# A conditional moved from between two stages to behind the last, with four vector sums and six weight loads re-spread

## The chip, the core and the metric

The kernel runs on one core of a Trainium2 chip. A core has five engines, each with its own instruction stream: TensorE (PE in the profile, its weight loads PEld), VectorE (DVE), ScalarE (ACT), GpSimd (POOL) and SyncE (SP). They meet through semaphores. DMAs are issued from the streams of SP, ACT and POOL and run on 16 DMA engines that all queues share. SP's DMAs form one queue: what is issued later lands later. The metric is the device time in microseconds (us) of one execution; lower is better.

## The reference

Two layers on `x` of 4 x 1024 tokens by 1024 channels (4096 tokens). Each layer gates its input with a two-way decayed scan over time (`_bi_wkv`); the first layer then applies a dense 1024 x 1024 product, the second an RMS norm and a mixture of experts: 32 experts with 4 chosen per token, plus one shared expert. Cut to what the change touches:

```python
logits = flat @ router_w.T
topk_w, topk_ids = lax.top_k(softmax(logits), 4)        # 4 experts for each token
gu = lax.ragged_dot(xs, w1, group_sizes)                # w1: 32 x 1024 x 1024
g, u = jnp.split(gu, 2, axis=-1)
ys = lax.ragged_dot(silu(g) * u, w2, group_sizes)       # w2: 32 x 512 x 1024
shared = (silu(flat @ sg) * (flat @ su)) @ sd           # the shared expert, all tokens
out = residual + (routed + shared)
```

All of it is float32.

## The kernel before

The 4096 tokens are cut into 8 chunks of 512. The kernel has three stages, each a stretch of straight-line code for every engine.

**Stage 1** (`run(order())`, line 932 on) makes the scans, the first layer, the router and the shared expert of chunks 0 to 5. TensorE's work there is a list of *pieces*, each an output tile of 128 x 512 that costs 16 matmul instructions: `first_ffn`, `shared_up` and `shared_down`. `run` (line 380) walks the list. For each piece it first issues the weight DMA of the piece two places further on (`early`), then the piece's matmuls (`do`), then whatever `after(n, ...)` has put n pieces later (a DVE pass that empties PSUM comes one piece later, the transposes back to rows two pieces later), and last one step of every generator in the list `beside`. The generators are the planner's side work: a bare `yield` ends a step. The order of the instructions on each engine is exactly this order of emission, because the whole stage stands in a `manual_schedule` block; nothing is moved later.

The last pieces are the sixteen of `shared_up(5)` (line 640) and the eight of `shared_down(5)` (line 667), called **U0 to U15** and **D0 to D7** here. D-piece ct loads 512 KB of `sd` weights (`wpc`, line 673, three buffers), loads the 256 KB residual tile `rT` (line 677), multiplies, lets DVE add the product into `rT` (line 694), transposes it (line 685), copies it (ACT, line 686) and writes it to `sum_d` (ACT's queue, line 687).

Beside these runs `plan` (line 705), which turns the router's choices into lists of tokens for blocks of one expert each, in *units*: a pair unit is two blocks of 128 tokens of one expert, a single unit one block. 68 pair and 12 single units are written out in the code (`WHOLE`); rarer inputs need further units. `plan` leaves the number of these further units in `many[2]`; in this input it is zero. Part-way, `plan` appends the generator `first_weights` (line 895), which loads the expert weights of the first two units: `load` (line 815) issues for a unit three DMAs of 2048 KB each on SP's queue, the two halves of `w1` (line 826, called **w1a** and **w1b** below) and `w2` (line 833). Steps of `first_weights` before: both halves of unit 0's `w1` after U14; its `w2` after U15; both halves of unit 1's `w1` after D0; its `w2` after D1.

Pair units multiply by a seven-product scheme that needs sums of weight quarters. `sums_up` (line 838, instructions at line 845) makes those of a unit's `w1` with four DVE subtractions over 128 x 2048 elements, which read both halves of `w1`. For unit 0 they stand after the end of the pieces (lines 938 and 939).

**Between the stages** (line 1243) stands `with tc.If(count(2, ...) > 0)`. Every engine loads `many[2]` into a register (line 1226), compares and branches. The body holds the further units (`extra`), and then loads the first two units' weights, unit 0's sums and unit 0's tokens again, since the further units used their places. With zero further units each engine jumps over it, and on the way brings its semaphores to the values that the body would have left; what comes behind waits for those.

**Stage 2** (`run_units`, line 1170) works through the 80 units: transposes of the gathered tokens (line 980, copied by ACT at line 981), the up products, the down products (line 1126 for pairs), and an accumulating scatter into `sum_d`. Unit 0's tokens were gathered during `plan`; those of unit 1 are gathered by POOL (line 878) when stage 2 starts.

**Stage 3**, at the end, makes the shared expert of chunks 6 and 7 (line 1421 on), copies finished rows of `sum_d` to `out`, and adds the last two chunks in SBUF (`sums[j]`, line 1463), from where ACT's queue writes them to `out` (line 1464).

Of the kernel before, what the change touches and what calls it, by code (L numbers as in the profile page):

```python
# [22 lines left out]
P = 128  # L23
CH = 512
# [7 lines left out]
def kernel(  # L32
# [15 lines left out]
    nc = tc.nc  # L48
# [5 lines left out]
    NT = B * T  # L54
# [9 lines left out]
    MAXU = (MAXB // 2, E)  # L64
    WHOLE = (68, 12)
# [11 lines left out]
    sum_d = dram.tile([NT + P, C], FP, name="sum_d")  # L77
# [11 lines left out]
        out=before, in_=before, pattern=[[1, P]], compare_op=ALU.is_gt, fill=0.0, base=0, channel_multiplier=-1  # L89
# [48 lines left out]
    for L in range(2):  # L138
# [7 lines left out]
        q = const.tile([P, NC, B], FP, name=f"rest{L}")  # L146
# [5 lines left out]
    with tc.tile_pool(name="empty", bufs=1) as pz:  # L152
# [9 lines left out]
            out=slots_d[0 : E * BPE * BLK, :].rearrange("(p r s) o -> p r s o", p=P, s=BLK), in_=nil  # L162
        )
        nc.sync.dma_start(
            out=slots_d[E * BPE * BLK :, :].rearrange("(p s) o -> p s o", p=1), in_=nil[0:1, 0, :, :]
        )

        for n in range((NT - 2 * CH) // P, NT // P, 2):
            nc.scalar.dma_start(
                out=sum_d[bass.ds(n * P, 2 * P), :].rearrange("(p r) c -> p (r c)", p=P), in_=zeros  # L170
# [192 lines left out]
    count, told = [0], [0]  # L363
# [16 lines left out]
    def run(pieces, ahead=2):  # L380
        for i, piece in enumerate(pieces):
            for p in pieces[i : i + ahead + 1]:
                if p.early:
                    p.early()
                    p.early = None
            while work["vector"] < pace[0] * work["tensor"] and mix():
                pass
            piece.do()
            work["tensor"] += piece.tensor
            count[0] += 1  # L390
            now = sorted(d for d in due if d[0] <= count[0])
            due[:] = [d for d in due if d[0] > count[0]]
            for _, _, f, vector, tensor in now:
                f()
                work["vector"] += vector
                work["tensor"] += tensor
            for stream in list(beside):
                step = next(stream, None)
                if step is None:
                    beside.remove(stream)  # L400
                else:
                    work["vector"] += step[0]
                    work["tensor"] += step[1]
# [51 lines left out]
    sums, accs = {}, {}  # L455
# [247 lines left out]
    have = {}  # L703

    def plan():
# [9 lines left out]
        with tc.tile_pool(name="plan", bufs=1, side="right") as pl, tc.tile_pool(  # L715
# [24 lines left out]
            for kind, n in enumerate((npair, nsing)):  # L740
# [50 lines left out]
                if kind == 0:  # L791
                    beside.append(first_weights())
# [17 lines left out]
    whole = []  # L810
# [4 lines left out]
    def load(unit, at):  # L815

        kind, n = unit
        e = nc.values_load(
            have["experts"][0:1, kind, n : n + 1],
            engines=[SP],  # L820
            min_val=0,
            max_val=E - 1,
            skip_runtime_bounds_check_because="worked out above from counts, and held to that range",
        )
        for k in range(2):
            nc.sync.dma_start(
                out=have["w1"][at][k],
                in_=w1[bass.ds(e, 1), k * NK * P : (k + 1) * NK * P].rearrange("e (k p) f -> p (e k) f", p=P),
            )
            if k == 0:  # L830
                yield
        yield
        nc.sync.dma_start(
            out=have["w2"][at], in_=w2[bass.ds(e, 1)].rearrange("e (k p) f -> p (e k) f", p=P)
        )
        yield

    def sums_up(at):


        (b11, b12), (b21, b22) = ((w[:, :, 0:I], w[:, :, I : 2 * I]) for w in have["w1"][at])
        t = have["t_up"]

        def op(to, x, y):
            nc.vector.tensor_tensor(to, x, y, ALU.subtract)  # L845

        op(t[3], b22, b12)
        yield
        op(b12, b12, b11)
        yield  # L850
        op(t[2], b22, b12)
        yield
        op(t[4], b21, t[2])
        yield
# [21 lines left out]
    def gather(to, i, n):  # L876

        nc.gpsimd.indirect_dma_start(  # L878
            out=to,
            out_offset=None,  # L880
            in_=h_d,
            in_offset=bass.IndirectOffsetOnAxis(ap=have["tokens"][:, i, n : n + 1], axis=0),
        )
        return to
# [8 lines left out]
        have["t_down"] = {i: pwt.tile([P, ND, 512], FP, name=f"t_down{i}") for i in (2, 3, 4)}  # L893

    def first_weights():
        for at in range(2):
            for step, _ in enumerate(load(whole[at], at)):
                if step == 1:
                    yield 0.0, 0.0
            yield 0.0, 0.0  # L900

    def order():

        pieces = first_ffn(0, False) + first_ffn(1, False) + late_gate(0)

        pieces.insert(-1, Piece(lambda: None, tensor=LATENCY / 3))
        pieces += [Piece(lambda: None, tensor=0.5) for _ in range(7)]

        def slower():
            pace[0] = PACE  # L910
            work["tensor"] = max(work["tensor"], work["vector"] / PACE)

        pieces.append(Piece(slower, tensor=0.0))
        up, gates = shared_up(0), late_gate(1)
        for i, piece in enumerate(up):
            pieces.append(piece)
            if i % 2 == 1:
                pieces.append(gates.pop(0))
        pieces += gates
        pieces += shared_down(0) + shared_up(1) + shared_down(1)  # L920
        pieces += first_ffn(2, True) + first_ffn(3, True) + shared_up(2) + shared_down(2) + shared_up(3)
        for b in range(2, B):
            q = NCH * b

            pieces += first_ffn(q, True) + first_ffn(q + 1, True)
            if b + 1 < B:
                pieces += shared_down(q - 1) + shared_up(q)
            else:
                pieces += shared_down(q - 2) + shared_up(q - 1) + shared_down(q - 1)
        return pieces  # L930

    with tc.manual_schedule(engines={PE, DVE, ACT, POOL, SP}):
        run(order())

        run([Piece(lambda: None, tensor=0.0) for _ in range(3)])
        while beside:
            run([Piece(lambda: None, tensor=0.0)])
        for _ in sums_up(0):
            pass

# [3 lines left out]
    with ExitStack() as m:  # L946
# [219 lines left out]
        def rest_of(s):  # L1166
            for _ in s:
                pass
# [54 lines left out]
        ENG = {PE, DVE, ACT, POOL, SP}  # L1223

        def count(at, most):
            return nc.values_load(
                many[0:1, at : at + 1],
                min_val=0,
                max_val=most,
                skip_runtime_bounds_check_because="a sum of counts, held to that range",  # L1230
            )

        def extra(kind, lo, n):
            if lo >= MAXU[kind]:
                return
            with tc.If(n > lo):
                us = [Unit((kind, i), i % 2) for i in range(lo, min(lo + 4, MAXU[kind]))]
                with tc.manual_schedule(engines=ENG):
                    run_units(us, False)
                extra(kind, lo + 4, n)  # L1240


        with tc.If(count(2, MAXU[0] + MAXU[1]) > 0):
            for kind in range(2):
                extra(kind, WHOLE[kind], count(kind, MAXU[kind]))
            with tc.manual_schedule(engines=ENG):
                for at in range(2):
                    rest_of(load(whole[at], at))
                rest_of(sums_up(0))
                for i, hs in enumerate(have["first"]):  # L1250
                    gather(hs, i, whole[0][1])

        tail = NT // CH - 2
# [90 lines left out]
        with tc.manual_schedule(engines=ENG):  # L1348
# [90 lines left out]
            sums = []  # L1439
            for j, w in enumerate(have["w1"][before_last]):  # L1440
                sums.append(w.rearrange("p k f -> p (k f)").rearrange("p (t c) -> p t c", c=C))
                nc.sync.dma_start(
                    out=sums[j], in_=sum_d[bass.ts(tail + j, CH), :].rearrange("(t p) c -> p t c", p=P)
# [39 lines left out]
            for m in range(HF):  # L1483
                i = NSI + m
# [15 lines left out]
                turn_out()  # L1500


# [1 line left out]
_VECS = {  # L1504
    "w0": "L0_cond_w",
# [52 lines left out]
```

## Time and profile before

| | |
|---|---|
| median of 3 runs | 5091.98 us (5087.41 to 5094.61) |
| the profiled execution | 5095.89 us |
| its span, first to last instruction | 5093.8 us |
| TensorE busy | 4793.8 us, 94% |
| VectorE busy | 3225.9 us, 63% |
| ScalarE, GpSimd busy | 1434.3 us, 811.1 us |
| DMA | 1071.45 MB, mean 210 GB/s |
| mean granted TensorE clock | 0.989 |

The profile gives for each engine the instructions in order of time, with the idle time before each and what ended it. A float32 matmul of 128 x 512 shows as two instructions of about 0.59 us that overlap, so that 16 of them take 7.03 us. Stage 2 begins at 1881.22 us from the start of the span, stage 3's last instruction on TensorE is at 5088.84 us. A row whose engine carries a q is of the engine's sequencer: it waits, branches or issues a DMA. The duration of an issued DMA in a row of SP is the time that SP needed to hand it to the queue, not the transfer's.

### The profile page before, as it was taken

How to read it: one execution, taken by the hardware profiler on the slowest of the kernel's cores; microseconds unless marked ns; L12 is line 12 of the kernel's file. 1: busy time of each engine (PE TensorE's matmuls, PEld its weight loads, DVE VectorE, ACT ScalarE, POOL GpSimd, SP SyncE). 2: the span in 40 equal slices, each digit the busy share in tenths (PEclk: the TensorE clock that was granted, in tenths of full speed). 3: DMA queues.
4: the chain of work that ended last, by engine and by line, in shares of the span. 5: the costliest groups of instructions: out<-in, count | busy, mean ns of one | idle time of the engine just before them, and what ended most of it. 6: DMA issues, size and time to landing. Idle time of an engine off the chain costs nothing.

```text
span 5093.8 us, 36409 instructions
## 1 busy us (share of the span) xinstructions
PE 4793.8 (94%) x12810; PEld 2220.2 (44%) x12810; DVE 3225.9 (63%) x3416; ACT 1434.3 (28%) x1833; POOL 811.1 (16%) x765
## 2 busy tenths in 40 slices
PE   0479999999899979999999999999999999999999
PEld 0124444444444434444444444444444444444444
DVE  9988988888752226565656565565656565656434
ACT  5557656566441101111111111111111111111100
POOL 0113202401222101111111111111111111111100
PEclk9979999999999989999999999999999999999999
DMA  4678679669678356767676767676767767676633
GB/s 156 188 203 217 189 227 278 165 203 285 176 204 229 118 196 218 232 220 232 217 238 215 238 214 239 216 237 216 237 215 238 225 228 225 227 226 226 183 110 108
DMA packets 502209, 1071.45 MB, mean 210 GB/s; under 512 B 30433, under 2 KB 235362, under 8 KB 501186
## 3 DMA queue, kind: packets, MB, share of 16 engines
q1 hardware_dynamic: 364050, 736.31, 41.9%
q0 software_dynamic: 74656, 223.12, 20.9%
q10 hardware_dynamic: 63312, 109.59, 6.0%
q8 instruction: 104, 1.70, 0.1%
q14 instruction: 87, 0.71, 0.0%
HBM read 833.65 MB, written 205.65 MB: 204 GB/s over the span
## 4 chain that ended last, share of the span: by engine, by line
PE 63%; ACT 0%; issue 0%; DVE 0%; ACTq 0%
PE gA L1126 15%; PE gC L1126 10%; PE gB L1126 10%; PE dA L1126 8%; PE dB L1126 5%; PE dC L1126 5%; PE tr L980 2%; PE gA L1014 2%; PE gB L1014 2%; PE tr L1063 1%; PE dA L1076 1%; PE dB L1076 1%; ACT hsT L981 0%; PE tr L1461 0%; ACT y L1083 0%
## 5 line engine op out<-in xcount | busy, mean ns | idle before, releaser
L652 PE MATMUL mm<-c,wpc 128*128 128x512 f32 x1536 | 667.1, 593 | 0.0
L440 PE MATMUL mm<-c,w0t 128*128 128x512 f32 x1024 | 450.0, 601 | 206.7 <-DMA w0t<-in_w 206.7
L1126 PE MATMUL gC<-w,s_up 128*128 128x512 f32 x1184 | 532.3, 592 | 0.0
L1126 PE MATMUL gB<-t_up,s_up 128*128 128x512 f32 x1152 | 517.9, 592 | 0.0
L1126 PE MATMUL gA<-w,hsT 128*128 128x512 f32 x1088 | 489.7, 593 | 0.0
L1110 POOL DMA_INDIRECT sum_d<-y,tokens x148 | 303.6, 2052 | 920.7 <-DMA sum_d<-y,tokens 545.5
L652 PEld LDWEIGHTS mm<-c,wpc 128*128 128x128 f32 x1536 | 289.6, 190 | 355.1 <-issue 353.9
L878 POOL DMA_INDIRECT hs<-h_d,tokens x146 | 147.6, 1011 | 1636.5 <-PE tr L980 1540.6
L440 PEld LDWEIGHTS mm<-c,w0t 128*128 128x128 f32 x1024 | 196.7, 193 | 456.1 <-issue 444.5
L680 PE MATMUL mm<-sact,wpc 128*128 128x512 f32 x768 | 345.3, 604 | 14.9 <-DMA wpc<-in_sd 12.2
L1126 PEld LDWEIGHTS gC<-w,s_up 128*128 128x128 f32 x1184 | 224.8, 190 | 282.2 <-issue 282.2
L1126 PEld LDWEIGHTS gB<-t_up,s_up 128*128 128x128 f32 x1152 | 218.9, 190 | 275.5 <-issue 259.5
L845 DVE TENSOR_TENSOR t_up<-w,w 128x2048 f32<-128x2048 f32 x136 | 310.6, 2284 | 0.0
L1126 PEld LDWEIGHTS gA<-w,hsT 128*128 128x128 f32 x1088 | 201.7, 190 | 227.9 <-issue 227.9
L293 DVE TENSOR_TENSOR_SCAN fg<-decay,tail,fg 128x1024 f32<-128x1024 f32 x128 | 292.7, 2328 | 0.0
L1126 PE MATMUL dB<-t_down,s_down 128*128 128x512 f32 x544 | 256.9, 595 | 0.1
L1126 PE MATMUL dA<-w,actT 128*128 128x512 f32 x544 | 255.8, 592 | 0.0
L1126 PE MATMUL dC<-w,s_down 128*128 128x512 f32 x544 | 255.7, 592 | 0.0
L981 ACT COPY hsT<-tr 128x512 f32<-128x512 f32 x296 | 172.7, 588 | 292.8 <-PE tr L980 292.8
L1126 PE MATMUL gA<-t_up,hsT 128*128 128x512 f32 x544 | 244.5, 592 | 0.0
L1051 ACT ACTIVATE act<-c 128x512 f32<-128x512 f32 x68 | 42.9, 630 | 708.9 <-DVE c L1047 708.9
L680 PEld LDWEIGHTS mm<-sact,wpc 128*128 128x128 f32 x768 | 146.3, 195 | 189.0 <-issue 185.0
(295 smaller groups left out, 6386.3 us busy)
## 6 DMA issues: line engine op xcount, KB each, us to landing
w<-in_w SPq DMA_DIRECT2D x240, 2048.0 KB
fg<-euk POOLq DMA_DIRECT2D x64, 512.0 KB
c_d<-r ACTq DMA_DIRECT2D x64, 512.0 KB
w0t<-in_w SPq DMA_DIRECT2D x64, 512.0 KB
c<-c_d SPq DMA_DIRECT2D x120, 256.0 KB
wpc<-in_sg SPq DMA_DIRECT2D x48, 512.0 KB
wpc<-in_su SPq DMA_DIRECT2D x48, 512.0 KB
wpc<-in_sd SPq DMA_DIRECT2D x48, 512.0 KB
```

The source lines that it names most:

```text
L293: nc.vector.tensor_tensor_scan(fg[:, m, ::-1], decay[L][:, ct, b : b + 1].to_broadcast([P, T]), fg[:, m, ::-1], tail[:, m : m + 1], ALU.mu ...
L440: nc.tensor.matmul(mm, lhsT=tiles[ot][:, it, :], rhs=c0s[it], start=(it == 0), stop=(it == NC - 1))
L652: nc.tensor.matmul(mm, lhsT=wts[f, n][:, kt, :], rhs=c1s[q, kt], start=(kt == 0), stop=(kt == NC - 1))
L680: nc.tensor.matmul(mm, lhsT=wts[ct][:, f, :], rhs=acts[q, f], start=(f == 0), stop=(f == NSI - 1))
L845: nc.vector.tensor_tensor(to, x, y, ALU.subtract)
L878: nc.gpsimd.indirect_dma_start(out=to, out_offset=None, in_=h_d, in_offset=bass.IndirectOffsetOnAxis(ap=have["tokens"][:, i, n : n + 1], a ...
L980: nc.tensor.transpose(tr[:, r, :], hs[:, bass.ts(4 * q + r, P)], ident)
L981: nc.scalar.copy(self.hsT[:, 4 * q : 4 * q + 4, b, :], tr)
L1014: nc.tensor.matmul(ps, lhsT=self.hsT[:, k, 0, :], rhs=w[k // NK][:, k % NK, bass.ts(n, I)], start=(k == 0), stop=(k == NC - 1),)
L1076: nc.tensor.matmul(ps, lhsT=self.actT[:, k, 0, :], rhs=w[:, k, bass.ts(n, 512)], start=(k == 0), stop=(k == NI - 1),)
L1110: nc.gpsimd.indirect_dma_start(out=sum_d, out_offset=bass.IndirectOffsetOnAxis(ap=tokens[:, i, self.n : self.n + 1], axis=0), in_=y, in_of ...
L1126: nc.tensor.matmul(ps, lhsT=x[:, k, :], rhs=w[:, k, :], start=(k == 0 and not more), stop=(k == half - 1), skip_group_check=more,)
```

## The change

`first_weights` now issues one DMA of 2048 KB in a step: unit 0's w1a after U14, its w1b after U15, its w2 after D0; then unit 1's w1a after D1, its w1b after D3, its w2 after D5. Beside unit 1's loads, one instruction of unit 0's `sums_up` is emitted in each step: after D1, D2, D3 and D4. The loop that made the four sums behind the pieces is gone.

The conditional is gone from between the stages. One with the same condition stands behind stage 3. Its body first writes the last two chunks' rows back to `sum_d`, then does the further units, then copies all of `sum_d` to `out`; loading the first weights again is no longer needed there. With zero further units it is jumped over.

```diff
     def first_weights():
-        for at in range(2):
-            for step, _ in enumerate(load(whole[at], at)):
-                if step == 1:
-                    yield 0.0, 0.0
+
+        for _ in load(whole[0], 0):
             yield 0.0, 0.0
+        sums = sums_up(0)
+        for _ in load(whole[1], 1):
+            for _ in range(2):
+                yield (0.0 if next(sums, sums) is sums else 2.3), 0.0
 
@@ at the end of stage 1
         run([Piece(lambda: None, tensor=0.0) for _ in range(3)])
         while beside:
             run([Piece(lambda: None, tensor=0.0)])
-        for _ in sums_up(0):
-            pass
 
@@ between stage 1 and stage 2
-        with tc.If(count(2, MAXU[0] + MAXU[1]) > 0):
-            for kind in range(2):
-                extra(kind, WHOLE[kind], count(kind, MAXU[kind]))
-            with tc.manual_schedule(engines=ENG):
-                for at in range(2):
-                    rest_of(load(whole[at], at))
-                rest_of(sums_up(0))
-                for i, hs in enumerate(have["first"]):
-                    gather(hs, i, whole[0][1])
-
@@ behind stage 3
+        with tc.If(count(2, MAXU[0] + MAXU[1]) > 0):
+            for j in range(2):
+                nc.sync.dma_start(
+                    out=sum_d[bass.ts(tail + j, CH), :].rearrange("(t p) c -> p t c", p=P), in_=sums[j]
+                )
+            for kind in range(2):
+                extra(kind, WHOLE[kind], count(kind, MAXU[kind]))
+            for q in range(NT // CH):
+                nc.sync.dma_start(out=out[bass.ts(q, CH), :], in_=sum_d[bass.ts(q, CH), :])
```

## The prediction

> **What bounds the kernel now.** I read the waits of TensorE first, in two windows: from 1700 to 1885 us (the end of stage 1 and the step to stage 2), and from 1885 to 4995 us (stage 2 and most of stage 3).
>
> ```profile
> PE mm L680 <- DMA wpc<-in_sd: 12.2, 1, 12.2
> PE tr L980 <- DVEq L1243: 11.5, 1, 11.5
> PE tk_ps L797 <- DVE tokens L800: 6.1, 3, 4.7
> ```
>
> ```profile
> PE tr L980 <- ACT hsT L981: 3.5, 12, 0.3
> PE tr L1063 <- ACT hsT L981: 2.2, 12, 0.2
> PE dA L1076 <- ACT actT L1064: 0.7, 1, 0.7
> ```
>
> From 1885 us on TensorE waits 6.4 us in 3110: it bounds stages 2 and 3, so what starts stage 2 earlier ends the kernel earlier by as much. Ahead of it stand three waits of 12.2, 11.5 and 4.7 us, all within the stretch that the change touches. TensorE's rows show where (start, duration, instruction, idle before and its end):
>
> ```profile
> 1788.18 7.03 PE L680 MATMUL mm<-sact,wpc 128*128 128x512 f32 x16
> 1807.39 8.69 PE L680 MATMUL mm<-sact,wpc 128*128 128x512 f32 x16 [12.18 <-DMA wpc<-in_sd]
> ...
> 1828.74 0.49 PE L797 MATMUL tk_ps<-ident,got 128*128 128x128 f32 x1 [4.73 <-DVE tokens L800]
> 1829.03 9.75 PE L680 MATMUL mm<-sact,wpc 128*128 128x512 f32 x16
> ...
> 1867.83 1.04 PE L685 MATMUL tr<-ident,rT 128*128 128x128 f32 x8
> 1869.11 0.66 PE L685 MATMUL tr<-ident,rT 128*128 128x128 f32 x4 [0.24 <-ACT rT L686]
> 1881.22 3.78 PE L980 MATMUL tr<-ident,t_down 128*128 128x128 f32 x16 [11.46 <-DVEq L1243]
> ```
>
> These are D0, D1, the planner's transposes, D3, the last transposes and stage 2's first. D1 and D3 take 8.69 and 9.75 us instead of 7.03: TensorE ran at half clock after the idle stretch. The windows 1797 to 1807 and 1827 to 1835 show a granted clock of 0.67 and 0.57 against 1.00, and DMA engines busy at 1.04 and 1.08 of what they can, with 365 GB/s. Undisturbed, D4 to D7 follow at 7.30 us each. So the D-pieces lose 12.2 + 4.7 of waiting and 1.7 + 2.7 of slow clock, 21.3 us, and the step to stage 2 loses 11.5.
>
> The cause of the first lies in SP's queue:
>
> ```profile
> 1787.05 1.00 SPq L826 DMA_DIRECT2D w<-in_w  x2
> 1788.09 0.51 SPq L673 DMA_DIRECT2D wpc<-in_sd  x1
> 1788.79 12.65 SPq L833 DMA_DIRECT2D w<-in_w  x1
> 1801.48 0.51 SPq L673 DMA_DIRECT2D wpc<-in_sd  x1
> 1802.04 7.15 SPq L677 DMA_DIRECT2D rT<-resT_d  x1
> ```
>
> D1's weights (1788.09) stand behind 4.19 MB of unit 0's `w1`, and `rT` of D0 and D1 behind more. DVE waits for `rT`, and the planner's copies stand behind it on DVE: that is the 4.7.
>
> **A rule for landings.** D1's weights landed at 1807.4; DVE went on with `rT` of D0, D1, D2 at 1815.0, 1827.7 and 1835.8. Bytes issued up to each since 1787.05, with the 1.18 MB of POOL's gathers at 1787 to 1792: 5.90, 8.78, 13.76, 16.64 MB. The estimate 1787.05 + MB / 0.375 + 4.4 us gives 1807.2, 1814.9, 1828.1, 1835.8. I use it below.
>
> **Part 1, the loads.** SP still waits for U15 until 1787.0 before the first. The new order is w1a, D1's weights, w1b, D2's weights, `rT` D0, w2, D3's weights, `rT` D1, unit 1's w1a, D4's weights, and so on. D1's weights have 3.80 MB at most before their end: 1801.6. TensorE is idle from 1795.2, so 6.4 us instead of 12.2. The wait is long enough for the slow clock once more, so D1 takes 8.7 again, to 1810.3. D2's weights (6.42 MB): 1808.6, in time. D3's (9.30 MB): 1816.3, needed at 1817.6, when D2 ends. `rT` of D1 (9.57 MB): 1817.0, so the planner's second transpose waits only for DVE's pass and copy, 0.75 + 0.28 and hand-overs, about 0.7 us, and D3 starts at 1818.9, warm. D4's weights (12.19 MB): 1824.0, needed at 1826.2. Then 7.30 each: D7's last matmul ends at 1855.0 instead of 1867.8. **Gain 12.9 us.** The margins are 1 to 2 us. Unit 1's w1b and w2, 4.19 MB, now come after D3 and D5, when the DMA was used at 0.32 (window 1835 to 1870), and are wanted only when DVE makes unit 1's sums (1899.8 before). `rT` of D6 and D7 stand behind the last w2, with a piece of slack.
>
> On the clock the Trainium skill ("TensorE: Matmul & The Clock Gate", Part 1) says that an idle window of about 3.4 us halves it and about 3.4 us of work restore it, 1.7 us lost each time. The rows show 1.7 and 2.7. By the page the old D-pieces lose 20.3 and the gain is 11.9; by the rows 12.9. I take the rows.
>
> **Part 2, the sums.** DVE's rows before:
>
> ```profile
> 1868.76 2.28 DVE L845 TENSOR_TENSOR t_up<-w,w 128x2048 f32<-128x2048 f32 x1
> 1871.07 2.29 DVE L845 TENSOR_TENSOR w<-w 128x2048 f32<-128x2048 f32 x1
> 1873.40 2.29 DVE L845 TENSOR_TENSOR t_up<-w,w 128x2048 f32<-128x2048 f32 x1
> 1875.72 2.29 DVE L845 TENSOR_TENSOR t_up<-w,t_up 128x2048 f32<-128x2048 f32 x1
> ```
>
> 4 x 2.3 = 9.2 us, with TensorE idle. They move behind DVE's passes of D0 to D3, one in a piece of 7.3 us, where DVE has 0.75 us and the planner's few copies to do. Cost nothing, covered by the matmuls. The first waits for w1b (5.90 MB, 1807.2), and its place on DVE comes at about 1811. Were w1b late, what stands behind it is the pass of D1 and the planner's copies, and TensorE waits for these; every us late beyond 1814 would be one on the path.
>
> **Part 3, the conditional between the stages.**
>
> ```profile
> L1243 PEldq COMPARE_BRANCH  x1: 3947/3947/3947, 1870.5 to 1870.5; - x1
> L1243 SPq COMPARE_BRANCH  x1: 50/50/50, 1857.5 to 1857.5; - x1
> L1243 ACTq COMPARE_BRANCH  x1: 50/50/50, 1873.0 to 1873.0; - x1
> L1243 DVEq COMPARE_BRANCH  x1: 72/72/72, 1876.8 to 1876.8; - x1
> ```
>
> DVE branches at 1876.8 and runs its next instruction at 1881.0: the jump costs 4.1 us, and TensorE waits for what comes behind it. ACT takes 2.5 between the same points, SP 2.5, TensorE 3.9 within the branch. All this goes. What is late next is ACT: after the last matmul (time 0) its three `rT` copies with their DMA issues run from 0.6 to 3.8, its four copies for stage 2 follow, and the transposes with two buffers wait for these. That puts the fourth transpose group's end, and the first up product, at 5.9 instead of 17.0 (1867.8 to 1884.8). That product runs warm: 3.43 instead of 3.88. **Gain 11.5 us**, sums included. Lower bound 7, if the first copies also wait about 4 us for the last `sum_d` write to land. POOL's gather for unit 1, held for 81.8 us by SP's part of the jump, may go at about 1793; its 1.05 MB then move the landings by 2.8 us, past margins of 1.3 to 2.2. I take **1 us** off for it (0 to 3).
>
> **Part 4, the conditional at the end.** Now it lies behind the last instruction. TensorE ends at 5089.5; five waits 0.5, the register load 0.76 (its row at 1869.6), the branch 3.95: 5094.7, and the semaphores 0.3. DVE: last instruction sent at 5089.5, then 0.5 + 0.55 + 0.07 + 4.1: 5094.8. ACT: last DMA issued at 5090.6, then 0.35 + 0.86 + 0.05 + 2.5: 5094.4. SP and POOL have long been there and jumped. The closing barrier takes 0.9 after the last. So 5096.1 instead of 5093.8 (there it waits for the last write, landed at 5092.6): **2.3 us lost**. Here a page weighs against the change: "Runtime: NRT & Kernel Launch", Instruction fetch mechanics, says that a taken branch out of the fetched window must fetch its target first; while "Advanced Engine Details and Errata", Control Flow Timing, prices a compare-and-branch at 108 ns. By the latter the end would cost nothing, hidden by the last write. The rows at line 1243 side with the former; bounds 0 and 6 (POOL's slowest jump took 6.1).
>
> **Sum.** 12.9 + 11.5 - 1 - 2.3 = 21.1 us, of the profiled 5095.89, so 5074.8 there. That execution is 3.9 above the median; on the median, 5091.98 - 21.1 = **5071 us**.
>
> **Rivals.**
> 1. *The burst stays.* The loads still want 2.88 MB in a piece of 7.3 us, 394 GB/s, and the windows show 365 to 386. If each of D1 to D4 misses its margin, the loads' gain halves to 5: 11.5 + 5 - 1 - 2.3 = 13, giving 5079. For it: the margins of 1 to 2 us. Against: unit 1's load now runs at half the rate.
> 2. *The old wait is replaced.* Stage 2's tiles lie where stage 1's did, and wait for the last `sum_d` write: boundary 7 instead of 11.5, giving 5076. For it: ACT's row at line 1140 waits for those semaphores. Against: that wait was over at once, and the first of it comes 9 us later.
> 3. *Slower.* DVE is in order, and the first sum stands ahead of D1's pass. If w1b lands at T, D3 cannot start before about T + 3.5, against 1818.9; the gain of 21 is gone from T = 1836 on, and with T = 1850 the kernel takes 5105. Against: the same bytes landed at 1807.
> 4. *It does nothing.* The gains meet something later that was due anyway, giving 5091. Against: TensorE's 6.4 us of waits in stages 2 and 3.
>
> **How the numbers follow.** Forecast 0.66 (own range 5064 to 5076), rival 1 0.13, rival 2 0.10, rival 3 0.05, rival 4 0.06. 0.2% is 10.2 us, about what a measurement of this kernel can tell. Faster: the forecast, rival 2 and most of rival 1, 0.86; within: rival 4 and the poor end of rival 1, 0.09; slower 0.05. The range leaves out rivals 3 and 4 and some of each tail: 5063 to 5081.
>
> **What would show it.** D1 waits about 6 us, D3 starts near 1819 without a wait over 1 us; four line-845 rows between 1810 and 1845; stage 2's first transposes near 1857 with no idle above 1; branches after 5065 with 2.5 to 4 us behind them, the span ending 5 to 7 us after the last transpose. A wait over 3 us of DVE for `w`, or a wait of TensorE at line 980 for a DMA, would prove me wrong.

## The result, and the profile after

The changed kernel takes 5075.59 us (median of 8 runs, 5070.53 to 5079.3), the one before in the same runs 5092.75 (8 runs, 5087.41 to 5096.23): a ratio of 0.9967, 95% interval 0.9956 to 0.9978, or 11 to 22 us. The forecast was 5071, with a range of 5063 to 5081. The profiled execution took 5070.53 us with a span of 5068.8, against 5095.89 and 5093.8: 25 us in these two.

The two longest waits of TensorE from 1700 to 1900 us (us in total, times, longest):

```profile
PE mm L680 <- DMA wpc<-in_sd: 7.4, 1, 7.4
PE tk_ps L797 <- DVE tokens L800: 1.7, 3, 0.9
```

The wait of 11.5 us for the jump at L1243 is gone, the planner's longest fell from 4.7 to 0.9, and D1's fell from 12.2 to 7.4. TensorE's rows of the same stretch:

```profile
1785.02 7.03 PE L680 MATMUL mm<-sact,wpc 128*128 128x512 f32 x16
1799.43 9.36 PE L680 MATMUL mm<-sact,wpc 128*128 128x512 f32 x16 [7.38 <-DMA wpc<-in_sd]
...
1817.10 0.39 PE L797 MATMUL tk_ps<-ident,got 128*128 128x128 f32 x1 [0.38 <-DVE tokens L800]
1817.32 7.03 PE L680 MATMUL mm<-sact,wpc 128*128 128x512 f32 x16
...
1853.41 1.04 PE L685 MATMUL tr<-ident,rT 128*128 128x128 f32 x8
1854.48 0.44 PE L980 MATMUL tr<-ident,t_down 128*128 128x128 f32 x2
1854.75 0.60 PE L685 MATMUL tr<-ident,rT 128*128 128x128 f32 x4
1855.19 0.82 PE L980 MATMUL tr<-ident,t_down 128*128 128x128 f32 x6
...
1857.78 3.60 PE L1126 MATMUL gA<-w,hsT 128*128 128x512 f32 x8
```

D1 still starts late and runs 9.36 us instead of 7.03, so the slow clock came once more (granted clock 0.51 from 1797 to 1804 us); D3 starts without a loss and runs 7.03 (granted clock 1.00 from 1804 on). From D0's first matmul to the last transposes of the D-pieces it is 1853.41 - 1785.02 = 68.39 us, where it was 1867.83 - 1788.18 = 79.65. The first up product follows 1857.78 - 1853.41 = 4.36 us later (16.96 before). What these rows also show is that L980, an instruction of stage 2, runs *between* two groups of L685, the last of stage 1. On ACT, too, a copy of stage 2 (L981) stands between two of stage 1 (L686):

```profile
1855.13 0.59 ACT L686 COPY rT<-tr 128x512 f32<-128x512 f32 x1 [0.49 <-ACT rT L686]
1855.61 0.59 ACT L981 COPY hsT<-tr 128x512 f32<-128x512 f32 x1
...
1856.16 0.58 ACT L686 COPY rT<-tr 128x512 f32<-128x512 f32 x1
```

SP's rows (for an issued DMA the second number is the time to hand it to the queue), and DVE's rows of the four sums:

```profile
1783.88 0.40 SPq L826 DMA_DIRECT2D w<-in_w  x1
1784.33 0.50 SPq L673 DMA_DIRECT2D wpc<-in_sd  x1
1785.05 4.03 SPq L826 DMA_DIRECT2D w<-in_w  x1
1789.12 4.16 SPq L673 DMA_DIRECT2D wpc<-in_sd  x1
```

```profile
1809.44 2.29 DVE L845 TENSOR_TENSOR t_up<-w,w 128x2048 f32<-128x2048 f32 x1
...
1817.73 2.28 DVE L845 TENSOR_TENSOR w<-w 128x2048 f32<-128x2048 f32 x1
...
1823.21 2.28 DVE L845 TENSOR_TENSOR t_up<-w,w 128x2048 f32<-128x2048 f32 x1
...
1826.08 2.28 DVE L845 TENSOR_TENSOR t_up<-w,t_up 128x2048 f32<-128x2048 f32 x1
```

D1's weights (1784.33) now stand behind w1a alone, and all four sums run under matmuls. At the end of the kernel the branches stand at L1492:

```profile
L1492 PEldq COMPARE_BRANCH  x1: 4138/4138/4138, 5062.5 to 5062.5; - x1
L1492 DVEq COMPARE_BRANCH  x1: 72/72/72, 5063.8 to 5063.8; - x1
L1492 ACTq COMPARE_BRANCH  x1: 50/50/50, 5064.5 to 5064.5; - x1
```

The last piece of DVE's work starts at 5062.07 and the span ends at 5068.8, 6.73 us later. Before, it started at 5089.51 and the span ended 4.33 us later. So the end of the span is 2.4 us longer. The metric takes in a little more than the span: 5095.89 - 5093.84 = 2.05 us before and 5070.53 - 5068.80 = 1.73 after, so in the metric 2.1 of these 2.4 us are left.

**One ruler for all runs.** I cut each profiled span at four points: D0's first matmul; the last transposes of the D-pieces (so the first length is "D-pieces"); the first up product of stage 2 ("step"); the start of DVE's last instruction (the length up to it is "stages 2, 3"); the end ("tail"). The sum of the four is the time from D0 to the end.

| kernel | D0 starts at | D-pieces | step | stages 2, 3 | tail | D0 to the end |
|---|---|---|---|---|---|---|
| before | 1788.18 | 79.65 | 16.96 | 3204.71 | 4.33 | 3305.65 |
| before, again | 1786.87 | 79.53 | 16.89 | 3204.72 | 4.32 | 3305.46 |
| changed | 1785.02 | 68.39 | 4.36 | 3204.29 | 6.73 | 3283.77 |
| changed, again | 1788.73 | 68.56 | 4.36 | 3204.28 | 6.68 | 3283.88 |
| 1 loads as before | 1790.84 | 78.71 | 4.38 | 3204.28 | 6.67 | 3294.04 |
| 2 sums behind the pieces | 1788.08 | 69.39 | 4.36 | 3209.62 | 6.93 | 3290.30 |
| 3 conditional between | 1787.53 | 68.15 | 11.39 | 3205.00 | 4.33 | 3288.87 |
| 4 D1's weights first | 1788.82 | 59.51 | 4.36 | 3204.28 | 6.89 | 3275.04 |
| 4 again | 1792.95 | 60.22 | 4.36 | 3204.30 | 6.72 | 3275.60 |
| 5 no conditional | 1788.38 | 67.68 | 4.36 | 3204.28 | 5.51 | 3281.83 |
| 6 short one at the end | 1787.09 | 69.01 | 4.36 | 3204.28 | 7.00 | 3284.65 |
| 7 short one between too | 1787.91 | 68.85 | 4.36 | 3204.30 | 6.68 | 3284.19 |

From D0 on the two profiles of one kernel agree within 0.2 us (0.6 for kernel 4). The 25.0 us between the first two profiles are 11.26 of D-pieces + 12.60 of step + 0.42 in stages 2 and 3 - 2.40 of tail = 21.88, and 3.16 of a D0 that started earlier. The 0.42 is the first up product, which no longer starts at half clock (3.60 us instead of 4.04). Between kernels with the same loads (changed, 2, 3, 5, 6 and 7) the D-pieces differ more, 67.7 to 69.4 us.

### The profile page after: what moved, and what is told of

Same layout as the page of the kernel before. It is cut to its first block, busy times and chain, and to the rows that moved or that the text cites. A ratio compares the mean times of both kernels' runs of the same rounds, so it can differ in the third digit from the quotient of the medians.

```text
span 5068.8 us, 36393 instructions
## 1 busy us (share of the span) xinstructions
PE 4784.5 (94%) x12810; PEld 2216.4 (44%) x12810; DVE 3226.9 (64%) x3416; ACT 1432.7 (28%) x1833; POOL 809.8 (16%) x765
## 4 chain that ended last, share of the span: by engine, by line
PE 89%; DVE 3%; DMA 3%; ACT 3%; issue 1%; POOL 0%; SPq 0%; ACTq 0%; POOLq 0%; DVEq 0%
PE gA L1126 15%; PE mm L652 11%; PE gC L1126 10%; PE gB L1126 10%; PE dA L1126 8%; PE mm L440 7%; PE mm L680 6%; PE dB L1126 5%; PE dC L1126 5%; PE tr L980 2%; PE gA L1014 2%; PE gB L1014 2%; PE tr L1063 1%; PE tr L541 1%; DMA xg<-in_xT 1%
## 5 line engine op out<-in xcount | busy, mean ns | idle before, releaser
L680 PE MATMUL mm<-sact,wpc 128*128 128x512 f32 x768 | 343.0, 601 | 10.3 <-DMA wpc<-in_sd 7.4
L981 ACT COPY hsT<-tr 128x512 f32<-128x512 f32 x296 | 172.5, 588 | 280.9 <-PE tr L980 280.9
```

The lines of the kernel that those rows point to most:

```text
L680: nc.tensor.matmul(mm, lhsT=wts[ct][:, f, :], rhs=acts[q, f], start=(f == 0), stop=(f == NSI - 1))
L981: nc.scalar.copy(self.hsT[:, 4 * q : 4 * q + 4, b, :], tr)
```

## The experiments

The theory: the loads, the sums and the jump each give what the prediction's parts say, and D0's start varies from run to run. The rivals: one of them gives nothing by itself, the gains lie in each other's shadow, or stage 1 became faster. Diffs are against the changed kernel. All but two of the kernels compute the whole; 5 and 6 leave the further units out, which this input doesn't need.

**1. The loads as before.**

```diff
-        for _ in load(whole[0], 0):
-            yield 0.0, 0.0
-        sums = sums_up(0)
-        for _ in load(whole[1], 1):
-            for _ in range(2):
-                yield (0.0 if next(sums, sums) is sums else 2.3), 0.0
+        for at in range(2):
+            for step, _ in enumerate(load(whole[at], at)):
+                if step == 1:
+                    yield 0.0, 0.0
+            yield 0.0, 0.0
+        for _ in sums_up(0):
+            yield 2.3, 0.0
```

> The changed kernel with the six loads back in the old steps (both halves of unit 0's w1 after U14, its w2 after U15, both halves of unit 1's w1 after D0, its w2 after D1) and the four sums after D2 to D5. My theory (the burst of loads makes the waits within the D-pieces, the step to stage 2 is a gain of its own): from D0's first matmul to D7's last about 79 us again (before 79.7, after 68.4), D1 waits about 12 us for its weights, the step from D7's last matmul to stage 2's first up product stays at 4.4 us, the whole is 11 us slower than the changed kernel, about 5086. Rival (the D-pieces gained because the sums and the conditional left their end, not because of the loads): the stretch stays near 68 us and the whole near 5075.

TensorE's waits from 1700 to 1900 us:

```profile
PE mm L680 <- DMA wpc<-in_sd: 11.9, 1, 11.9
PE tk_ps L797 <- DVE tokens L800: 5.8, 3, 4.5
```

(The four sums come after D2 to D5 here.) The waits of the kernel before are back, the D-pieces take 78.71 us, and the time is 5087.17 (12 runs), 0.9985 [0.9977, 0.9994] of before. The step stays at 4.38. So the spread of the loads is worth 78.71 - 68.39 = 10.3 us by itself, and it does not touch the step.

**2. The sums behind the pieces, without a conditional there.**

```diff
-        sums = sums_up(0)
         for _ in load(whole[1], 1):
             for _ in range(2):
-                yield (0.0 if next(sums, sums) is sums else 2.3), 0.0
+                yield 0.0, 0.0
@@ behind the pieces
+        for _ in sums_up(0):
+            pass
```

> The changed kernel with unit 0's four sums behind the pieces again, where they were; the loads spread, the conditional at the end. My theory (sums and conditional lay one behind the other on DVE, but TensorE can do its transposes and the first product beside the sums): the first up product still starts 4.4 us after D7, the second waits for DVE until about 11.7 us after D7 instead of 7.8, so 4 us slower than the changed kernel, up to 6 with a dip of the clock: 5080. Rival (all of the sums' 9.2 us lies on the path): first product at 13 us or later, 9 us slower, 5085.

TensorE's rows after the step (lines behind the edit stand one further down in this kernel):

```profile
1861.84 3.60 PE L1127 MATMUL gA<-w,hsT 128*128 128x512 f32 x8
1868.80 5.40 PE L1127 MATMUL gB<-t_up,s_up 128*128 128x512 f32 x8 [3.36 <-DVE s_up L995]
```

The first product needs no sum and comes as early as in the changed kernel; the second waits 3.36 us for DVE and then runs 5.40 us instead of 3.60. It starts 11.3 us after the last transposes of the D-pieces; 11.7 was expected. The wait and the slow product are 5.2 us, and stages 2 and 3 are 5.3 us longer. The time is 5079.63 (7 runs), 0.997 [0.9959, 0.9981] of before.

**3. The conditional between the stages**, with the body of before and without the one at the end; loads and sums as in the changed kernel.

```diff
+        with tc.If(count(2, MAXU[0] + MAXU[1]) > 0):
+            for kind in range(2):
+                extra(kind, WHOLE[kind], count(kind, MAXU[kind]))
+            with tc.manual_schedule(engines=ENG):
+                for at in range(2):
+                    rest_of(load(whole[at], at))
+                rest_of(sums_up(0))
+                for i, hs in enumerate(have["first"]):
+                    gather(hs, i, whole[0][1])
@@ behind stage 3
-        with tc.If(count(2, MAXU[0] + MAXU[1]) > 0):
...
```

> The changed kernel with the conditional back between the stages with its old body, and none at the end; the loads and the sums as changed. My theory (the jump by itself costs TensorE about 6 us there: DVE's last pass 1.0, waits and register load 1.1, jump 4.1, then transposes 3.6): first up product about 10.6 us after D7 instead of 4.4, some 0.4 of slow clock, the end 2.4 us shorter, together 4 us slower than the changed kernel, 5080. Rival (the sums alone made the old step long, the jump was covered by them): first product at 5 to 6 us after D7, the end 2.4 shorter, 1 to 2 us faster than the changed kernel.

```profile
1855.68 1.04 PE L685 MATMUL tr<-ident,rT 128*128 128x128 f32 x8
1856.96 0.65 PE L685 MATMUL tr<-ident,rT 128*128 128x128 f32 x4 [0.24 <-ACT rT L686]
1863.47 3.81 PE L980 MATMUL tr<-ident,t_down 128*128 128x128 f32 x16 [5.86 <-ACTq L1243]
1867.07 4.31 PE L1126 MATMUL gA<-w,hsT 128*128 128x512 f32 x8
```

Two earlier rows, D1 on TensorE and POOL's first gather for unit 1, are used further down:

```profile
1800.88 10.17 PE L680 MATMUL mm<-sact,wpc 128*128 128x512 f32 x16 [6.32 <-DMA wpc<-in_sd]
1862.85 0.94 POOL L878 DMA_INDIRECT hs<-h_d,tokens  x1 [70.50 <-SPq L1243]
```

The step is 11.39 us instead of 4.36, and the first product runs 4.31 us instead of 3.60; the tail is 4.33 again. Between D0 and the end that is 5.1 us over the changed kernel. The time is 5077.91 (6 runs), 0.9968 [0.9955, 0.998] of before, 2.3 us over the changed kernel's median, which the intervals don't separate from 5. Of the 12.60 us by which the change shortened the step, 7.03 are the conditional's, and the other 5.57 the sums', near the 5.3 of experiment 2. How the 7.03 divide between the jump and the order that the conditional forces on the engines, no run shows.

**4. D1's weights ahead of all of unit 0's.** One more step before the first load moves the six loads one piece later; D1's weights are then issued before w1a.

```diff
     def first_weights():
+        yield 0.0, 0.0
         for _ in load(whole[0], 0):
             yield 0.0, 0.0
```

> The changed kernel with one empty step ahead of the first load, so that each load comes one piece later and D1's weights are issued ahead of unit 0's w1a. My theory (D1's wait of 7.4 us and the 2.3 us of slow clock behind it come from the one load that still stands ahead of D1's weights): no wait over 1.5 us in the D-pieces, from D0's first matmul to D7's last 59 to 61 us instead of 68.4, the rest as in the changed kernel, 8 to 9 us faster than it: 5067. Rival (the DMA engines are simply full, the wait moves to D2 or D3, or to the sums waiting for w1b): the stretch stays at 66 us or more and the gain below 3 us.

```profile
1788.82 13.90 PE L680 MATMUL mm<-sact,wpc 128*128 128x512 f32 x32
...
1802.96 7.14 PE L680 MATMUL mm<-sact,wpc 128*128 128x512 f32 x16
...
1812.02 0.39 PE L797 MATMUL tk_ps<-ident,got 128*128 128x128 f32 x1 [1.37 <-DVE tokens L800]
```

D0 and D1 are one block of 32 matmuls in 13.90 us: no wait, no slow clock (granted clock 1.00 throughout). D1's weights were issued at 1779.83 here, w1a at 1787.68. The D-pieces take 59.51 us, and the time is 5065.85 (4 runs, 5061.85 to 5074.8), 0.9947 [0.993, 0.9964] of before, whose median beside it was 5094.43. **From D0 on, this version is shorter than both kernels.** It was run once more:

> The version that issues the weights of D1 ahead of both halves of unit 0's w1, once more. If its gain over the changed kernel was not chance: the D-pieces take 59 to 61 us, and the time is 8 to 9 us below the changed kernel's, 5064 to 5068 us. If it was a favourable set of runs: 5070 to 5076 us.

The D-pieces took 60.22 us. The total, 5069.85 (4 runs), fell between the two expectations, beside 5096.19 for the kernel before: 0.995 [0.9933, 0.9966], close to the first ratio. D0 started at 1792.95 in this profile, the latest of all; from D0 on it is 8.2 to 8.8 us shorter than the changed kernel both times. In the trace, then, the gain was not chance; the total carries the start of D0 with it, and in the totals alone the intervals of this version and of the changed kernel (0.9956 to 0.9978) still overlap.

**5. No conditional at all.** The block behind stage 3 is taken out; the further units cannot be done.

```diff
-        with tc.If(count(2, MAXU[0] + MAXU[1]) > 0):
...
-            for q in range(NT // CH):
-                nc.sync.dma_start(out=out[bass.ts(q, CH), :], in_=sum_d[bass.ts(q, CH), :])
```

> The changed kernel without any conditional: it leaves out the further units, of which this input has none. My theory (the conditional at the end costs what the span shows behind DVE's last instruction, 6.7 us against 4.3): 4.3 us from DVE's last instruction to the end, 2.4 us faster than the changed kernel, 5073. Rival (the span's end is not the execution's: the closing costs elsewhere what it saves here): the tail shrinks but the time stays, 5075 to 5076.

The tail is 5.51 us, not 4.3: only half of the 2.4 us comes back. The other 1.2 us are there without any conditional. The time is 5075.82 (6 runs, 5072.02 to 5080.53), 0.9964 [0.9951, 0.9976], which lies where the rival had it but scatters too much to decide. What the execution takes outside the span was 2.48 us in the profiled execution (1.75 to 2.63 in the six runs) against 1.73 in the changed kernel, so part of what the tail saves does come back there, as the rival says.

**6. A short conditional at the end.** The body loses the further units (`extra`) and keeps ten writes, so that the jump is over a few instructions.

```diff
-            for kind in range(2):
-                extra(kind, WHOLE[kind], count(kind, MAXU[kind]))
```

> The changed kernel with the conditional at the end, but only the writes of sums and the copies to the output in its body; the further units, of which this input has none, are left out, so the jump is over a few hundred bytes of code instead of all units. My theory (the 3.5 to 4 us behind each branch are the fetch of a target far away): the branch of TensorE takes below 0.5 us, the gap behind DVE's and ACT's below 0.5, the tail is 4.5 to 5 us. Rival (a taken branch costs that much wherever it leads): TensorE's branch takes about 4 us and the tail stays at 6.7.

```profile
L1492 PEldq COMPARE_BRANCH  x1: 369/369/369, 5065.2 to 5065.2; - x1
```

The branch fell from 4.14 us to 0.37, as expected, and yet the tail is 7.00 us, not the 4.5 to 5 expected (5073.44 us, one run). So a long jump is not needed for a long tail. The transfers of the last 8 us say what is there besides. In the following rows each number is the rate in a slice of 0.2 us, in GB/s; the last slice is the span's end. The kernel before:

```profile
GB/s 0 0 18 271 289 289 294 149 0 0 0 0 0 0 0 0 0 0 0 0 0 0 184 289 289 261 269 302 289 287 287 164 0 0 0 0 0 0 0 0
```

The changed kernel, with two queues of the same view:

```profile
GB/s 0 0 0 0 0 0 0 0 0 0 248 289 284 230 305 353 271 269 264 95 20 31 100 10 5 20 23 8 0 0 0 0 0 82 41 41 0 0 0 0
...
q14 instruction: 5, 0.04, 1.7%
q8 instruction: 2, 0.03, 1.6%
```

Experiment 6, and then 5:

```profile
GB/s 0 0 0 0 0 0 0 0 20 274 287 279 246 310 271 274 269 330 51 23 20 8 8 10 8 20 23 13 0 0 0 0 0 0 0 0 0 0 0 0
```

```profile
GB/s 292 133 0 0 0 0 0 0 0 0 0 0 0 0 0 0 202 292 289 253 266 302 289 279 289 182 0 13 5 0 0 0 0 0 0 0 0 0 0 0
```

Before, the last write's bulk ends at once, in slice 32. In the changed kernel the bulk ends in slice 20, and then 1.6 us follow at mostly 5 to 31 GB/s (the 100 has two of the code packets named below in it); in experiment 6 some 2 us at 8 to 51; in 5, two slices. 289 GB/s over 16 DMA engines is 18 for one: the trickle looks like one engine of the 16 that finishes late. The queues marked `instruction` carry, by that name, code: packets of 8 and 16 KB, seven in these 8 us of the changed kernel, two in experiment 6, one in experiment 5 and none in the kernel before; the trace has the 16 KB ones at 0.93 to 1.1 us. In experiment 6 both fall into the last write (starts 5066.42 and 5067.21). That the last write waits behind a code packet on its DMA engine is likely from these times, but no run had the one without the other.

Which of the two ends the tail can be read from the DRAIN rows, with which each engine goes into the closing barrier (first and last start). The changed kernel, then experiment 6:

```profile
L1548 SPq DRAIN  x3: 7/7/13, 5067.9 to 5068.2; - x3
L1548 DVEq DRAIN  x2: 10/14/17, 5067.6 to 5068.3; - x2
```

```profile
L1546 SPq DRAIN  x3: 7/7/7, 5070.9 to 5071.1; - x3
L1546 ACTq DRAIN  x2: 8/8/8, 5067.3 to 5071.2; - x2
```

SP is the one that waits for the last write, and it is last both times. In the changed kernel DVE, the last of the engines behind a long jump, is only 0.3 us ahead of it, so jumps and write run side by side and either alone would have made most of the 2.4 us. In experiment 6 the other engines are 3.6 us ahead, and SP with the late write makes the whole tail. Of SP's 2.4 us in the changed kernel, 1.6 are the later landing (3.6 us after the hand-over to the queue instead of 2.0); the other 0.8 are the conditional's semaphores, through which SP steps behind it: the span ends 2.0 us after the landing, where it was 1.3.

**7. A short conditional between the stages**, beside the one at the end.

```diff
+        with tc.If(count(2, MAXU[0] + MAXU[1]) > 0):
+            nc.vector.tensor_copy(many[:, 0:1], many[:, 0:1])
```

> The changed kernel, with a second conditional between the stages that has the same condition and a body of one small copy on VectorE, so that every engine loads the register, compares and branches there, but over a few instructions only. Theory A (the length of the jump is what cost the time between the stages): TensorE's branch there takes under 0.5 us, the first up product of stage 2 starts 5.5 to 7.5 us after D7's last matmul (4.4 without a conditional, 11.4 with the long jump), and the clock stays full. Theory B (any conditional there costs it, by the meeting of the engines and the semaphores): 10 us or more and half clock after it. The rest is as in the changed kernel: some 5073 to 5077 us by A, 5078 to 5082 by B.

```profile
L1242 PEldq COMPARE_BRANCH  x1: 241/241/241, 1843.3 to 1843.3; - x1
```

TensorE's branch took 0.24 us and the step 4.36, with 5073.82 us in one run. But neither theory was tested where it was meant to be: the row stands at 1843 us, among the D-pieces. Presumably because its body needs nothing of the last pieces, the conditional came to lie between them and separates nothing. The D-pieces with it take 68.85 us, against 68.39 and 68.56. What the run shows is that a short conditional which holds nothing back cost nothing that can be seen; what one would cost at the seam stays open.

**8. Both kernels once more.**

> The kernel before once more, for a second profile. The medians moved by 17 us, the two profiles of before and after by 21.9 us within the stretch that the change touches and 3.2 us ahead of it. If the rest is the start of D0, which varies from execution to execution (1785.0 to 1790.8 in six profiles): D0 to D7 again 79 to 80 us, first up product 17.0 us after D7, the tail 4.3. If the first profile showed a long case: D0 to D7 76 us or less.

> The changed kernel once more, for a second profile and more times. If the rest of the gain is in the start of D0: D0 to D7 68 to 69 us again, first up product 4.4 us after D7, the tail 6.7 to 6.9, and D0 later than 1785.0. If the first profile showed a short case: D0 to D7 72 us, with a wait of D2 or D3 for its weights.

From D0 on the new profiles repeat the first within 0.2 us: 3305.46 - 3283.88 = 21.6 us. The changed kernel took 5074.66 (6 runs, 5074.01 to 5078.24), beside 5094.0 for the one before: 0.9965 [0.9952, 0.9977], 12 to 24 us.

## Why the prediction was right, and where it wasn't

The direction and the mechanism held: 21.9 us between D0 and the end, where the sum had 21.1. That the total came so close was in part luck: the loads gave 1.6 us less than their term and the step 1.5 us more, and the two errors cancelled.

- **The loads: 12.9 predicted, 11.3 measured** (10.3 by undoing them alone). The D-pieces were to take 1855.0 - 1788.2 = 66.8 us and take 68.4. D1 was to wait 6.4 and waited 7.4; it was to run 8.7 and ran 9.36. D1's weights were due 13.4 us after D0's start by the landing rule and came at 14.4. What the rule left out is probably POOL's gather (see below). The margins of D2 to D4 held, so rival 1 didn't come about (its "halves to 5" should have been 6.5, half of 12.9). The 1.7 us of slow clock that the prediction puts down to the page on the clock gate are an estimate, half of the page's 3.4 us at half clock; D1 lost 1.6 to 3.1 us in the profiles in which it waited, so the rows were the better guide. What the old D-pieces lost was right: without any stall they would take 59.51 - 1.37 = 58.1, so they lost 21.5 (21.3 in the prediction).
- **The sums: cost nothing, right.** All four run between 1809 and 1828 under the matmuls, none waited for w1b (rival 3), and experiments 2 and 3 price them at 5.3 and 5.6 us where they stood.
- **The step: 11.5 predicted, 13.05 measured** (12.60, and 0.45 for a warm product). The first up product was to come at 5.9 us and came at 4.36. The prediction took the order on ACT as written: three `rT` copies with their DMAs, then the four for stage 2. That failed. With no conditional between them the two scheduled blocks met, and ACT's rows have L981 at 1855.61 between L686 at 1855.13 and at 1856.16; TensorE's rows show the same. That this order is worth the 1.5 us is the natural reading; no run kept the old order without a conditional. The section on the kernel before says that nothing is moved from the order of emission: that holds within the stage, not at this seam. The lower bound of 7 (rival 2, a wait for the last `sum_d` write) did not occur: no such wait is in the rows.
- **POOL's gather: 1 us predicted, likely but not proven.** It did go early, earlier than thought: two gathers ran at 1776.71 and 1787.54, the first ahead of the burst. In experiment 3, whose conditional held these gathers until 1862.85, D1 waited 6.32 us, as the landing rule had it; in the six profiles with the same loads and early gathers it waited 7.2 to 8.4. Against it: in experiment 1 the gather is early too, and D1 waits no longer than before (11.86 and 12.18). Taken together, loads less gather, the forecast was 11.9 and the measured gain 11.3.
- **The end: 2.3 predicted, 2.4 measured, by another sum.** The branch of TensorE was to take 3.95 and took 4.14. But the prediction had the last write long landed; it landed 3.6 us after it was handed to the queue (2.0 before), and SP, which waits for it, was the last into the barrier, 0.3 us behind DVE. Experiments 5 and 6, with no jump and with a short one, have tails of 5.5 and 7.0 with a late write. So the branch path was forecast about right and a second one as long was missed. Of the two notes that were weighed, the Trainium skill's "Runtime: NRT & Kernel Launch", Instruction fetch mechanics (a jump out of the fetched code waits for its target), agrees with the rows: 4.14 us for the long jump, 0.37 and 0.24 for short ones. The 108 ns of "Advanced Engine Details and Errata", Control Flow Timing, is the price of none of TensorE's branches here.
- **The median.** 21.9 us between D0 and the end became 17.2 between the medians (11 to 22), and 19.3 in the second set (12 to 24). Both intervals take in 21.6 to 21.9. D0 starts between 1785.0 and 1793.0 in the twelve profiles, in no order by kernel, so stage 1 before D0 moves a total by several us. That the change itself makes stage 1 longer by a few us isn't excluded; what in stage 1 varies I could not place.

## What to carry to other kernels

A conditional that is never taken is paid for by the distance it jumps and probably by the order it fixes: this one cost 7.0 us between two stages. Moved behind the last instruction it left an end 2.4 us longer than before, of which 1.2 stayed when it was taken out altogether. Where one queue carries bulk loads and the next tile's weights, put the small urgent load ahead of the whole bulk: that one step of order was worth 8 us on top of thinning the burst. And when a total scatters by 10 us, compare lengths between two fixed instructions of the trace, which here repeat to 0.2 us for most kernels and 0.6 for one.

## What the hardware showed unexpectedly

A jump of TensorE over the further units takes 3.9 to 4.1 us, over ten writes 0.37, over one copy 0.24. What seems to be the fetching of code shows as DMA packets of 8 and 16 KB on queues of their own, and the landing of the last write beside them was 0.9 to 1.9 us later than where there were none; even without the conditional, one such packet came at the end, and the tail was 5.5 us instead of 4.3.
